# Bringing a recurrent state back to token layout: DVE 32x32 squares and a trip through DRAM in place of PE transposes

## The chip, the core and the metric

The kernel runs on one core of a Trainium2 chip. The metric is the device time of one launch in microseconds (us), of which the profiler gives a span (first to last instruction) and, for each engine, what it did when. The engines are named as in the profile: PE (TensorE, matrix multiply), PEld (its weight loads, which run beside the multiplies), DVE (VectorE), ACT (ScalarE), POOL (GpSimd) and SP (SyncE, which here only issues DMAs). Each engine works through its own list of instructions in order and waits on semaphores for the others.

## The reference

Four graph layers are applied to 32 graphs of 512 nodes with 128 features, all float32, over one adjacency matrix `adj` of 512x512. Each is `x = x + layer(relu(layernorm(x)))`. Layer 0 is a graph convolution, layer 1 a gated recurrent network of five steps, layers 2 and 3 are attention layers. The change touches layer 1 alone:

```python
def step(h, _):
    m_in = jnp.einsum('nm,bmd->bnd', in_matrix, h)      # both matrices are adj here
    m_out = jnp.einsum('nm,bmd->bnd', out_matrix, h)
    av = jnp.concatenate([m_in, m_out], axis=-1)
    u3 = h @ u3_w.T + u3_b
    z = jax.nn.sigmoid(av @ w3_w.T + w3_b + u3)
    r = jax.nn.sigmoid(av @ w4_w.T + w4_b + u3)
    hv = jnp.tanh(av @ w5_w.T + w5_b + (r * h @ u5_w.T + u5_b))
    h = (1.0 - z) * h + z * hv
    return (h, None)
h, _ = jax.lax.scan(step, input, None, length=5)
...
h = jnp.maximum(_layernorm(x, axis=-1), 0.0)
x = x + _L1_gnn_ref(h, adj, adj, ...)
```

The state `h` of a graph is 512 nodes by 128 features. The product with `adj` sums over nodes, the gates sum over features.

## The kernel before

**Layouts.** TensorE sums over partitions, so the state is kept twice: in token layout `h` (partition = node within a block of 128, then 4 blocks, then 128 features; C = 4 blocks) for the product with `adj`, and in feature layout `hT` (partition = feature, then 512 nodes) for the gates. The recurrence itself is computed in feature layout; `hT` has to be brought back to token layout once per step, for the next step's product, and after the last step for the sum `x += h - 1` (the 1 is taken off here because the elu of the next layer is added further on without its -1).

**A step of the recurrence** is four functions. `ggnn_prod` (L227) multiplies `h` as the stationary operand by `adjT` in four accumulating matmuls of 512 columns (L189) and copies the sum to `m` on ACT (L231). `ggnn_reset` (L234) runs two matmuls for the reset gate (L237, L238), tanh on ACT (L240) and one DVE operation giving `rh` (L242). `ggnn_update` (L245) adds to the same PSUM bank for the update gate (L247), tanh on ACT (L249), runs two matmuls for the candidate (L251, L252; the second needs `rh`), tanh on ACT (L254), then three DVE operations (L255, L256, L258), of which the last writes the new `hT`. `ggnn_back` (L261) brings it back to tokens: four TensorE transposes of 128x128 into the PSUM bank `back` (L264, recorded at the helper's line L184), and either an ACT copy to a new `h` (L267) or, after the last step, a DVE operation that adds it to `x` (L272).

**Order.** The order is written out at the end of the function (L344 to L364). Time is divided into slots `t`. Each slot holds one step of one graph (its product), the gates of the graph whose product was in the slot before, and the return to tokens of the graph whose product was two slots before; four graphs (LANES) are in flight, and a graph's next product comes four slots after the last one. Beside that each slot has pieces of the other layers (the list `side`): per graph the graph convolution (`gcn_in`, `gcn_prod`, `gcn_out`), the entry to the recurrence (`ggnn_in`, `ggnn_turn`), and for each of the two attention layers `gat_in`, `gat_heads`, `gat_edges`, `gat_out`. Five slots make a period, after which one more graph is through. Only in the first and last dozen slots are some of them empty. The framework in which it is written builds each engine's list from this and may move instructions against each other by its own planning; buffers rotate in pools: seven for `h`, eight for `hT`, two for a work tile where nothing is said, two PSUM banks called `side`, one tile of two banks called `wide`.

**What else is used below.** `ggnn_in` (L215) writes the first `h` with four ACT operations (L179). `ggnn_turn` (L220) transposes it to `hT` on TensorE (L184, `side<-ident,h`). `gat_heads` transposes its input (L184, `side<-ident,y`), copies it on DVE (L293, `gT`), and multiplies it (L296, `wide`). The output of a graph leaves by one DMA on SP's queue (L340).

Of the kernel before, what the change touches and what calls it, by code (L numbers as in the profile page):

```python
# [8 lines left out]
F32 = mybir.dt.float32  # L9
BF16 = mybir.dt.bfloat16  # L10
AF = mybir.ActivationFunctionType
ALU = mybir.AluOpType

P = 128
EPS = 1e-5
STEPS = 5
SLOPE = 0.2
LANES = 4


@with_exitstack
def gnn_stack(ctx: ExitStack, tc: tile.TileContext, a: dict, out: bass.AP):
    nc = tc.nc
    x, adj = a["x"], a["adj"]
    B, N, D = x.shape
    C = N // P
# [7 lines left out]
    def bank(name, bufs=1):  # L34
        return psum.tile([P, C, P], F32, name=name, bufs=bufs)

    def side_bank():
        return bank("side", 2)
# [4 lines left out]
    def flat(t):  # L43
        return t.rearrange("p c k -> p (c k)")
# [32 lines left out]
    xs = []  # L77
# [12 lines left out]
    for m in range(C):  # L90
        p = side_bank()
# [20 lines left out]
    for m in range(C):  # L112
        nc.vector.scalar_tensor_tensor(anT[:, m, :], anT[:, m, :], dinv[:, m:m + 1], flat(drow),
                                       op0=ALU.mult, op1=ALU.mult)
# [31 lines left out]
    for l in (2, 3):  # L146
# [5 lines left out]
        p = side_bank()  # L152
# [4 lines left out]
    work = ctx.enter_context(tc.tile_pool(name="work", bufs=2))  # L157
# [15 lines left out]
    def norm_relu(b, y):  # L173

        mv, rstd = norm_stats(b)
        off = stat.tile([P, C], F32, name="off")
        nc.vector.scalar_tensor_tensor(off, mv[:, :, 0], -1.0, rstd, op0=ALU.mult, op1=ALU.mult)
        for c in range(C):
            nc.scalar.activation(y[:, c, :], xs[b][:, c, :], AF.Relu, bias=off[:, c:c + 1],  # L179
                                 scale=rstd[:, c:c + 1])  # L180

    def to_features(p, y):
        for c in range(C):
            nc.tensor.transpose(p[:, c, :], y[:, c, :], ident)  # L184

    def product(p, h, mT):

        for c in range(C):
            nc.tensor.matmul(flat(p), h[:, c, :], mT[:, c, :], start=(c == 0), stop=(c == C - 1))  # L189

    kept = {}


# [19 lines left out]


    def ggnn_in(b):  # L215
        h = work.tile([P, C, D], F32, name="h", bufs=LANES + 3)
        norm_relu(b, h)
        kept["h", b] = h

    def ggnn_turn(b):  # L220
        p = side_bank()
        to_features(p, kept["h", b])
        hT = work.tile([P, N], F32, name="hT", bufs=2 * LANES)
        nc.scalar.copy(hT, flat(p))
# [20 lines left out]
    def ggnn_update(b, s):  # L245
# [10 lines left out]
        nc.vector.scalar_tensor_tensor(hv, z, 1.0, hv, op0=ALU.add, op1=ALU.mult)  # L256
        new = work.tile([P, N], F32, name="hT", bufs=2 * LANES)
        nc.vector.scalar_tensor_tensor(new, hv, 0.5, hT, op0=ALU.mult, op1=ALU.add)  # L258
        kept["hT", b] = new

    def ggnn_back(b, s):  # L261
        hT = kept["hT", b]
        p = bank("back")
        to_features(p, hT.rearrange("p (c k) -> p c k", c=C))  # L264
        if s < STEPS - 1:
            h = work.tile([P, C, D], F32, name="h", bufs=LANES + 3)
            nc.scalar.copy(flat(h), flat(p))  # L267
            kept["h", b] = h
        else:
            del kept["hT", b]  # L270

            nc.vector.scalar_tensor_tensor(flat(xs[b]), flat(xs[b]), -1.0, flat(p), op0=ALU.add, op1=ALU.add)  # L272

# [67 lines left out]

    span = LANES * (STEPS - 1)  # L344
    side = [(-8, gcn_in), (-7, gcn_prod), (-6, gcn_out), (-5, ggnn_in), (-4, ggnn_turn)]
    for i, l in enumerate((2, 3)):
        for k, f in enumerate((gat_in, gat_heads, gat_edges, gat_out)):
            side.append((span + 3 + 4 * i + k, lambda b, f=f, l=l: f(b, l)))

    def turn(t):  # L350
        s = -t % STEPS
        b, rest = divmod(t - LANES * s, STEPS)
        return (b, s) if rest == 0 and 0 <= b < B else None
# [3 lines left out]
    for t in range(first, last + 1):  # L357
        for lag, f in ((1, ggnn_reset), (0, ggnn_prod), (2, ggnn_back), (1, ggnn_update)):
            if (i := turn(t - lag)) is not None:
                f(*i)  # L360
        for k, f in side:
            b, rest = divmod(t - k, STEPS)
            if rest == 0 and 0 <= b < B:
                f(b)  # L364
# [30 lines left out]
```

The softmax here doesn't subtract the row's maximum and nothing guards it: scores larger than these inputs give would overflow.

## Time and profile before

| | |
|---|---|
| runs | 1884.26 us median of 3 (1883.15 to 1886.05) |
| profiled execution | 1884.31 us, span 1882.5 us |
| PE busy | 1832.7 us, 97% of the span |
| PEld busy | 1052.9 us, 56% |
| DVE busy | 1039.3 us, 55% |
| ACT busy | 723.8 us, 38% |
| POOL busy | 184.7 us, 10% |
| DMA, all queues | 19.88 MB, mean 11 GB/s |
| granted TensorE clock | 0.992 |

Busy times are of the whole span, with overlaps of one engine's instructions counted once. A float32 matmul appears as two records, a transpose as one. The recorded duration of a matmul runs past the start of the next, since they are pipelined: the time that one takes of the engine is the distance from its start to that of the next. After a vertical bar the tables of groups give busy time and mean duration, and after a second bar the engine's idle time just ahead of the group with what ended it.

### The profile page before, as it was taken

Reading aid. Unit: us, or ns where it says so; the run is one execution under the profiler, and the core shown is the slowest. Engines: PE = TensorE matmul, PEld = TensorE weight load, DVE = VectorE, ACT = ScalarE, POOL = GpSimd, SP = SyncE. Lnnn points to the kernel's source line nnn. Section 1 sums busy time; section 2 is a strip of 40 time slices with the busy share of each in tenths; the row PEclk is TensorE's granted clock in tenths of the full one; section 3 lists DMA queues with packets and bytes.
Section 4 is the critical chain, followed back from the end, with each engine's and each line's share of the span. In section 5 each row is a group of like instructions: output and inputs, shape, how many; then the busy total and the mean of one; then the engine's idle time right before and its main releaser. Section 6 shows DMA issues by size and latency. Waiting matters only on the chain.

```text
span 1882.5 us, 19768 instructions
## 1 busy us (share of the span) xinstructions
PE 1832.7 (97%) x7264; PEld 1052.9 (56%) x7264; DVE 1039.3 (55%) x2814; ACT 723.8 (38%) x1453; POOL 184.7 (10%) x168
## 2 busy tenths in 40 slices
PE   4999999999999999999999999999999999999995
PEld 2444556555556555556555556555555555555664
DVE  3334565555565555555565556565556565555665
ACT  2444443443343444343444344344344344333321
POOL 1101010110010111011111011111011011000000
PEclk9999999999999999999999999999999999999997
DMA  8000000000000000000000000000000000000000
GB/s 218 1 1 1 0 6 7 6 1 6 6 6 7 6 1 6 6 6 7 6 1 6 6 6 6 6 1 6 7 6 7 6 1 6 6 6 6 6 12 12
DMA packets 37056, 19.88 MB, mean 11 GB/s; under 512 B 2528, under 2 KB 36448, under 8 KB 36960
## 3 DMA queue, kind: packets, MB, share of 16 engines
q1 hardware_dynamic: 34368, 17.83, 3.3%
q8 instruction: 57, 0.93, 0.2%
q10 hardware_dynamic: 2592, 0.79, 0.2%
q14 instruction: 39, 0.32, 0.1%
HBM read 10.23 MB, written 8.39 MB: 10 GB/s over the span
## 4 chain that ended last, share of the span: by engine, by line
PE 96%; DVE 2%; DMA 1%; ACT 1%; issue 0%; POOL 0%; SPq 0%; ACTq 0%; DVEq 0%; POOLq 0%
PE prod L189 29%; PE wide L323 12%; PE gate L247 7%; PE cand L252 7%; PE gate L237 7%; PE cand L251 7%; PE gate L238 7%; PE side L189 6%; PE back L184 4%; PE wide L296 3%; PE side L184 2%; PE side L211 2%; PE side L311 1%; DMA x<-in_x_dram 1%; DMA u<-in_L_gnn_u_w_dram 0%
## 5 line engine op out<-in xcount | busy, mean ns | idle before, releaser
L189 PE MATMUL prod<-adjT,h 128*128 128x512 f32 x1280 | 583.2, 594 | 0.0
L189 PEld LDWEIGHTS prod<-adjT,h 128*128 128x128 f32 x1280 | 240.4, 191 | 285.7 <-issue 285.6
L255 DVE TENSOR_TENSOR hv<-hv,hT 128x512 f32<-128x512 f32 x160 | 111.0, 694 | 481.8 <-ACT hv L254 481.8
L170 POOL TENSOR_TENSOR rstd<-ve,mhalf 128x4 f32<-128x4 f32 x128 | 129.4, 1011 | 1557.4 <-DVE off L282 973.0
L323 PEld LDWEIGHTS wide<-h_gat,e 128*128 128x128 f32 x2048 | 238.3, 193 | 20.5 <-issue 11.6
L323 PE MATMUL wide<-h_gat,e 128*128 128x129 f32 x2048 | 241.8, 276 | 3.5 <-DVE o L338 1.5
L231 ACT COPY m<-prod 128x512 f32<-128x512 f32 x160 | 93.1, 582 | 328.6 <-PE prod L189 328.6
L240 ACT ACTIVATE r<-gate,gate_bw 128x512 f32<-128x512 f32 x160 | 109.9, 687 | 277.4 <-PE gate L238 273.6
L314 DVE SCALAR_TENSOR_TENSOR e<-side,h_gat,maskT 128x512 f32<-128x512 f32 x256 | 183.6, 741 | 4.2 <-PE side L311 4.0
L242 DVE SCALAR_TENSOR_TENSOR rh<-r,hT 128x512 f32<-128x512 f32 x160 | 109.4, 684 | 106.2 <-ACT r L240 106.0
L237 PE MATMUL gate<-m,w4T 128*128 128x512 f32 x320 | 164.2, 595 | 2.0 <-ACT m L231 1.5
L247 PE MATMUL gate<-m,w3T 128*128 128x512 f32 x320 | 164.3, 595 | 0.2 <-ACT r L240 0.2
L252 PE MATMUL cand<-rh,u5T 128*128 128x512 f32 x320 | 163.5, 592 | 0.3 <-DVE rh L242 0.3
L238 PE MATMUL gate<-hT,u3T 128*128 128x512 f32 x320 | 163.4, 592 | 0.0
L251 PE MATMUL cand<-m,w5T 128*128 128x512 f32 x320 | 163.4, 592 | 0.0
L254 ACT ACTIVATE hv<-cand,gate_bw 128x512 f32<-128x512 f32 x160 | 109.1, 682 | 97.2 <-PE cand L252 96.8
L258 DVE SCALAR_TENSOR_TENSOR hT<-hv,hT 128x512 f32<-128x512 f32 x160 | 134.7, 842 | 2.6 <-DVE arg L298 0.2
L184 PEld LDWEIGHTS back<-ident,hT 128*128 128x128 f32 x640 | 79.8, 141 | 84.8 <-issue 81.9
L285 ACT ACTIVATE y<-x,off 128x128 f32<-128x128 f32 x256 | 87.7, 393 | 92.7 <-DVE off L282 92.7
L249 ACT ACTIVATE z<-gate,gate_bw 128x512 f32<-128x512 f32 x160 | 109.5, 684 | 27.9 <-PE gate L247 27.9
L164 DVE BATCH_NORM_STATS2 st<-x 128x6 f32<-128x128 f32 x512 | 119.0, 280 | 1.2
L189 PE MATMUL side<-anT,y 128*128 128x512 f32 x256 | 117.4, 601 | 1.9 <-ACT y L179 1.9
(93 smaller groups left out, 1625.8 us busy)
## 6 DMA issues: line engine op xcount, KB each, us to landing
x<-in_x_dram SPq DMA_DIRECT2D x32, 256.0 KB, 5.4
out_dram<-o SPq DMA_DIRECT2D x32, 256.0 KB, 2.2
adj_sb<-in_adj_dram SPq DMA_DIRECT2D x4, 256.0 KB, 5.3
w<-in_L_gnn_w_w_dram ACTq DMA_DIRECT2D x3, 128.0 KB, 5.6
u<-in_L_gnn_u_w_dram ACTq DMA_DIRECT2D x2, 64.0 KB, 4.5
w<-in_L_gnn_W_dram ACTq DMA_DIRECT2D x1, 64.0 KB, 3.0
b<-in_L_gnn_b_dram ACTq DMA_DIRECT2D x1, 64.0 KB, 5.4
w_aug<-in_L_gnn_W_dram ACTq DMA_DIRECT2D x1, 64.0 KB, 3.7
```

The lines of the kernel that those rows point to most:

```text
L164: nc.vector.bn_stats(st[:, c, :], xs[b][:, c, :])
L170: nc.gpsimd.tensor_tensor(rstd, ve, mhalf, ALU.pow)
L184: nc.tensor.transpose(p[:, c, :], y[:, c, :], ident)
L189: nc.tensor.matmul(flat(p), h[:, c, :], mT[:, c, :], start=(c == 0), stop=(c == C - 1))
L237: nc.tensor.matmul(flat(p), wT["w4"], m, start=True, stop=False)
L238: nc.tensor.matmul(flat(p), wT["u3"], hT, start=False, stop=True)
L247: nc.tensor.matmul(flat(p), wT["w3"], m, start=False, stop=True, skip_group_check=True)
L251: nc.tensor.matmul(flat(q), wT["w5"], m, start=True, stop=False)
L252: nc.tensor.matmul(flat(q), wT["u5"], rh, start=False, stop=True)
L258: nc.vector.scalar_tensor_tensor(new, hv, 0.5, hT, op0=ALU.mult, op1=ALU.add)
L314: nc.vector.scalar_tensor_tensor(e[:, j, :], flat(row), h[:, j, D + 1:D + 2], maskT[l][:, j, :], op0=ALU.max, op1=ALU.mult)
L323: nc.tensor.matmul(p[:, c, :D + 1], e[:, j, c * P:(c + 1) * P], h[:, j, :D + 1], start=(j == 0), stop=(j == C - 1))
```

## The change

The return to token layout leaves TensorE. DVE transposes `hT` in squares of 32x32 within each group of 32 partitions, which puts each feature group's squares into `sq`; four DMAs, one for each group of 32 partitions, write `sq` to a scratch tensor in DRAM in which the four feature groups of a token stand side by side; a fifth DMA reads that as the new `h`. All five are on SP's queue, and the fifth waits for the four. The tile `h` now has the features outside and the four blocks inside, so that a block's features are 16 bytes apart for all who write or read it: the ACT operations of `ggnn_in`, the stationary operand of the product and of `ggnn_turn`, and the sum at the end. That sum now reads `h` from SBUF and no longer a PSUM bank.

```diff
+W = 32
+Q = P // W
...
+    dram = ctx.enter_context(tc.tile_pool(name="dram", bufs=1, space=bass.MemoryType.DRAM))
+
+    def to_tokens(h, hT):
+        sq = work.tile([P, Q, W, C], F32, name="sq")
+        nc.vector.transpose(sq.rearrange("p q j c -> p q c j"), hT.rearrange("p (c q i) -> p q c i", c=C, q=Q))
+        d = dram.tile([Q, W, Q, W * C], F32, name="squares", bufs=4)
+        for a in range(Q):
+            nc.sync.dma_start(d[:, :, a, :].rearrange("q i k -> i q k"),
+                              sq[a * W:(a + 1) * W].rearrange("i q j c -> i q (j c)"))
+        nc.sync.dma_start(h.rearrange("p j c -> p (j c)"), d.rearrange("q i a k -> (q i) (a k)"))
...
     def ggnn_in(b):
-        h = work.tile([P, C, D], F32, name="h", bufs=LANES + 3)
+        h = work.tile([P, D, C], F32, name="h", bufs=LANES + 3).rearrange("p d c -> p c d")
         norm_relu(b, h)
...
     def ggnn_back(b, s):
         hT = kept["hT", b]
-        p = bank("back")
-        to_features(p, hT.rearrange("p (c k) -> p c k", c=C))
+        h = work.tile([P, D, C], F32, name="h", bufs=LANES + 3)
+        to_tokens(h, hT)
+        h = h.rearrange("p d c -> p c d")
         if s < STEPS - 1:
-            h = work.tile([P, C, D], F32, name="h", bufs=LANES + 3)
-            nc.scalar.copy(flat(h), flat(p))
             kept["h", b] = h
         else:
             del kept["hT", b]
-            nc.vector.scalar_tensor_tensor(flat(xs[b]), flat(xs[b]), -1.0, flat(p), op0=ALU.add, op1=ALU.add)
+            nc.vector.scalar_tensor_tensor(xs[b], xs[b], -1.0, h, op0=ALU.add, op1=ALU.add)
```

In the changed file the lines lie 14 or 15 lower: the square is L199, the writes L202, the read L204, the last sum L286.

## The prediction

> **What bounds the kernel now.** First the page's busy shares and its chain of work that ended last:
>
> ```profile
> PE 1832.7 (97%) x7264; PEld 1052.9 (56%) x7264; DVE 1039.3 (55%) x2814; ACT 723.8 (38%) x1453; POOL 184.7 (10%) x168
> ...
> PE 96%; DVE 2%; DMA 1%; ACT 1%; issue 0%; POOL 0%; SPq 0%; ACTq 0%; DVEq 0%; POOLq 0%
> ```
>
> PE is the bound, and a busy PE can still hide gaps, so I read one period (five slots) in the timeline of PE. It starts at 1000.13 and the next at 1056.40: 56.27 us without a gap, five times with the work that the change removes:
>
> ```profile
> 1001.85 3.60 PE L189 MATMUL prod<-adjT,h 128*128 128x512 f32 x8
> 1005.28 0.60 PE L184 MATMUL back<-ident,hT 128*128 128x128 f32 x4
> 1005.72 1.02 PE L247 MATMUL gate<-m,w3T 128*128 128x512 f32 x2
> ...
> 1032.02 1.06 PE L296 MATMUL wide<-w_aug,gT 128*128 128x131 f32 x8
> ...
> 1039.36 1.02 PE L252 MATMUL cand<-rh,u5T 128*128 128x512 f32 x2
> ```
>
> A group of four transposes holds PE from 1005.28 to 1005.72, 0.44 us. A time taken off PE is therefore a gain as long as DVE still delivers `gT` before 1032.02, `rh` before 1039.36, and so on. DVE's timeline of the same period:
>
> ```profile
> 1005.92 0.69 DVE L272 SCALAR_TENSOR_TENSOR x<-x,back 128x512 f32<-128x512 f32 x1 [0.63 <-PE back L184]
> ...
> 1009.40 0.69 DVE L255 TENSOR_TENSOR hv<-hv,hT 128x512 f32<-128x512 f32 x1 [1.33 <-ACT hv L254]
> ...
> 1014.43 0.69 DVE L242 SCALAR_TENSOR_TENSOR rh<-r,hT 128x512 f32<-128x512 f32 x1 [2.88 <-ACT r L240]
> ...
> 1030.92 0.69 DVE L293 COPY gT<-side 128x512 f32<-128x512 f32 x1 [0.99 <-PE side L184]
> ...
> 1037.72 0.67 DVE L242 SCALAR_TENSOR_TENSOR rh<-r,hT 128x512 f32<-128x512 f32 x1
> ```
>
> `gT` is done at 1031.61, 0.41 us ahead of its matmul; the last `rh` at 1038.39, 0.97 ahead. Between 1030.92 and 1037.72 DVE has no idle time: this stretch, not its 55%, decides. For the DMAs, two rows of issues:
>
> ```profile
> out_dram<-o SPq DMA_DIRECT2D x32, 256.0 KB, 2.2
> adj_sb<-in_adj_dram SPq DMA_DIRECT2D x4, 256.0 KB, 5.3
> ```
>
> The first is a store on an idle queue, the second a load like the new one (128 rows of 2 KB) with three others in flight; its fastest took 2.9 us.
>
> **What the skill says.** *VectorE: DVE Perf Modes*, "The three transpose paths": DVE transposes squares of 32x32 only, 311 ns for 128x128 bf16. *SBUF — State Buffer*, "Specifications (TRN2)": cache lines of 16 bytes need two hits for full bandwidth; the new `sq` and `h` are walked at a step of 16 bytes, one hit each. No row of before walks a large tile so. *TensorE: Matmul & The Clock Gate*, "What happens when you issue a matmul": weight loads are pulled ahead of running matmuls, at columns/1.2 ns, 107 ns for 128; the trace's transposes stand 0.44/4 = 0.109 us apart, which agrees. Its Part 1 says that PE's clock halves after some 3.4 us of idling: after a wait of 4.1 us at 41.02 the stretch from 40 to 60 us has a mean clock of 0.84, against 1.00 before it.
>
> **The change part by part.** All against the profiled execution, 1884.3 us (span 1882.5 and 1.8 around it), which is the median of the runs to 0.05 us.
>
> *Removed from PE.* 160 groups; 2 lie where the head waits and 6 in the tail after 1775 us (counted below), so 152 x 0.438 = **-66.6 us**. Also 128 ACT copies (L267, 592 ns, 75.7 us): nothing by themselves, ACT is idle 62% of the time. The bank `back` is of no use to others.
>
> *The square on DVE, 160.* For contiguous data 311 ns + 384 further elements: L338 (344 ns for 128 elements, PSUM input) and L133 (291 ns) against 691 ns for 512 put one element near 1.0 ns, so about 0.69 us, the price of any 128x512 operation here. At half rate on the 16-byte write side, 0.16 fixed + 512 x 2.08 ns = 1.22 us. Both ends stay; I take 1.22, from the page's remark. In a dense stretch neighbours lasting 0.69 start 0.60 apart, so a square adds 0.60 to 1.13. By the built order one square falls between DVE's `hv` at 1020.82 and `gT` at 1030.92, where DVE's own work ends at 1029.92: +1.13 gives 1031.05. PE asks for `gT` 0.44 earlier than before, 1030.48. DVE is 0.57 late, 0.41 is to spare, and the weight load after `gT` needs some 0.2: PE waits 0.36 per period. About 30 periods: **+11 us** (0 at 0.69). The next square stands behind the last `rh`, and that keeps 0.3 of its 0.97. The three others fall into idle time of 0.7 to 2.9 us.
>
> *The trip.* SP issues in 0.372 us each (the store's issue): the fourth write starts 1.12 after the square, lands at most 2.2 later; the read takes 2.9; hand-overs 0.1: 6.3 us, from 5 (smaller writes land sooner) to 9 (the load's 5.3). For steps one to four the product comes some 20 us after the square in the built order, so it is hidden with 13 to spare; SP is otherwise idle, and one trip in five has a store of an output between its writes (1.3 us). After the last step DVE itself waits: square 999.6 to 1000.8, data at 1007.1, where the sum (L286) before began at 1005.92. Queued behind it: layer norm statistics, `hv`, and `rh` at 1014.43. The 1.33 and 2.88 us of idle time ahead of these take it up; from the start of L286 to that `rh` DVE has 6.7 us of work (L286 at half rate 1.22, statistics 1.6, three operations 2.1, a square 1.13, `rh` 0.69) and PE wants it near 1018.0 (1019.04 before, two groups of transposes earlier now, less the weight load), so L286 may start at 1011.3 and the trip last 10.5 us. Cost 0.
>
> *Strided `h`.* Each of a slot's 8 weight loads for the product has a matmul record of 0.43 us (3.43/8) over it; at half rate, 0.21 us, it stays hidden. `ggnn_turn`'s four transposes are only as long as their loads: +0.11 each, 3 exposed, 30 graphs: **+10 us** (0 at full rate). ACT's four writes of 494 ns grow by 0.13 at most, in the place of the copies removed.
>
> *The head.* In the first slots there is little to hide a trip behind. The first new `hT` was done at 62.78 and its product began at 64.17. Now 62.8 + 1.2 + 6.3 = 70.3, and by the built list an `anT` matmul stands ahead of the product and waits for DVE's statistics until about 71: 7 us late, of which 1.3 is filled with a turn and that matmul, and PE's clock costs some 2 after the gap: 8. The product at 82.49 waits likewise: its read stands on SP's queue behind two writes of the next square (about 93.5), so it lands near 97, while PE has work until 92.3: 5 with the clock's 1.5, less the idle 1.1 that this stretch had. With two returns saved **+13 us** (8 to 20).
>
> *The tail.* After 1775 us the slots are half empty, and three places wait for a return; I followed the built lists of PE and DVE through them with the durations above. DVE is in order: L286 waits for its trip, and `hv`, the next square, and `gT` for the attention layer stand behind it. The product of the 31st graph's last step and the attention work around it, done 30.1 us after the 30th's last candidate matmul, come to 34.2 (+4.1); the 32nd graph's last product +2.8; the last sum (back at 1835.82, L272 at 1836.85) comes 8 us later, but DVE's work for the other graph runs first and the matmuls after it move by 2.5. With 0.6 for the clock **+10 us** (6 to 18; each us more of trip costs 1 to 3 here and 2 in the head).
>
> Sum: -66.6 + 11 + 10 + 13 + 10 = -22.6; **1861.7 us**, 1.2% faster.
>
> **The rivals.**
> *A, no price for the step of 16 bytes:* squares 0.69, loads hidden: -66.6 + 12 + 8.6 = -46, **1838 us**. For it: the page gives no size of the penalty. Against: the remark itself.
> *B, dear weight loads, slower:* the step makes a load of `h` four times as long. In 30 periods the turns lose 90 x (L - 0.109) us, and the products 1200 x (L - 0.43) beyond 0.43. With the rest as forecast the gain of 22.6 (and the 10 that the turns have in it) is gone at L = 0.43 us: 90 x 0.32 = 29 and a little. At 0.45 it is 1861.7 - 10 + 31 + 24, **1906 us**. For it: nothing in this trace loads weights at a step. Against: PEld is 56% busy and idle for 285.7 us ahead of the product's 1280 loads, 0.22 each.
> *C, the trip stops DVE:* beyond 10.5 us each further us costs 32; at 11.2 the gain is gone, at 12 **1910 us**. Against: the store lands in 2.2 us, the queues are empty.
> *D, squares slower than half rate:* 1.9 us would give 0.7 more per period, and **1883 us**.
> That PE keeps its work cannot be: the built list has no such transposes.
>
> **How the numbers follow.** Forecast 0.52, A 0.24, B 0.08, C 0.06, D 0.05 and a head and tail at their upper ends together with the forecast's costs 0.05 (1876). Forecast and A are faster; C and most of B slower; D near the border. By the 0.2% (3.8 us) that a measurement of this kernel can tell: faster 0.77, same 0.05, slower 0.18. The forecast's own range is 1846 to 1877; with A below and D above, 1834 to 1888.
>
> **What would show it.** Right: a PE period near 54.4 us (56.27 - 2.19 + 0.36) with no `back`; squares near 1.2 us; issue of the first write to landing of the read near 6; L286 waiting about 1 us on a DMA; PE waits on a DMA of `h` only before 100 and after 1775 us; waits of `wide` (L310) on `gT`. Wrong: transposes of `ggnn_turn` or the products standing further apart (B); `hv` or `rh` late after L286 (C); long squares (D). The forecast is most easily spoiled by the size of the 16-byte penalty, which nothing here measures.

## The result and the profile after

The changed kernel takes 1885.36 us (median of 4 runs, 1883.74 to 1886.61) against 1884.17 for the kernel before: a ratio of 1.0005, with a 95% interval of 0.9987 to 1.0022. The forecast of 1861.7 us did not come. TensorE did lose its 160 groups of transposes, and the span is still 1882.0 us instead of 1882.5.

First the page of the changed kernel: the busy times, the chain, the row of the square with its mean duration after the comma, and the DMA issues with the time to landing in the last column.

```profile
PE 1786.1 (95%) x6624; PEld 1147.9 (61%) x6624; DVE 1194.8 (63%) x2974; ACT 663.4 (35%) x1325; POOL 172.5 (9%) x168
...
PE 68%; DVE 19%; issue 5%; POOL 3%; ACT 3%; DMA 1%; SPq 0%; DVEq 0%; ACTq 0%; POOLq 0%
...
L199 DVE STREAM_TRANSPOSE sq<-hT 128x512 f32<-128x512 f32 x160 | 175.9, 1100 | 1.3
...
squares<-sq SPq DMA_DIRECT2D x640, 64.0 KB, 1.8
h<-squares SPq DMA_DIRECT2D x160, 256.0 KB, 2.6
```

PE's share of the chain fell from 96% to 68%, and DVE's rose from 2% to 19%: the end is now set in part by work that PE waits for. One period of PE's timeline, to be read against the one shown of the kernel before:

```profile
1001.16 3.60 PE L191 MATMUL prod<-adjT,h 128*128 128x512 f32 x8
1004.59 1.02 PE L262 MATMUL gate<-m,w3T 128*128 128x512 f32 x2
...
1022.23 1.06 PE L310 MATMUL wide<-w_aug,gT 128*128 128x131 f32 x8
1023.12 2.85 PE L191 MATMUL prod<-adjT,h 128*128 128x512 f32 x6
1025.81 1.02 PE L262 MATMUL gate<-m,w3T 128*128 128x512 f32 x2
...
1036.17 1.02 PE L266 MATMUL cand<-m,w5T 128*128 128x512 f32 x2
1038.26 1.12 PE L267 MATMUL cand<-rh,u5T 128*128 128x512 f32 x2 [1.08 <-DVE rh L257]
```

No transposes stand after the product any more. The period lasts 55.56 us (the mean over a hundred products in the middle), 0.71 less than the 56.27 of before, where five groups of 0.438 should have given 2.19. Two losses are in these rows. The six records of the product after `wide` take 2.69 us (1023.12 to 1025.81) where they took 2.58 in the kernel before (1024.69 to 1027.27, two rows further down). And `cand<-rh` could have started at 1036.17 + 0.86 = 1037.03 and starts at 1038.26, 1.23 late (the row says 1.08, since the recorded end of a matmul runs past the next start); a weight load exposed behind this wait adds 0.11. Together that is 1.45, and 1.48 with 0.03 for the turn: what the period lacks. The two rows of the kernel before:

```profile
1024.69 2.74 PE L189 MATMUL prod<-adjT,h 128*128 128x512 f32 x6
1027.27 0.60 PE L184 MATMUL back<-ident,hT 128*128 128x128 f32 x4
```

In all, PE of the changed kernel waits for `rh` 27 times, about once a period; the columns are total, count and longest:

```profile
PE cand L267 <- DVE rh L257: 27.3, 27, 1.1
...
PE prod L191 <- DMA h<-squares: 4.3, 1, 4.3
```

Over the whole run, from the starts of the 160 products compared with before: the fourth product is 15.6 us late (what comes up to it is the head), the 157th is 13.9 early (so the middle gained 29.5 of the 67 that 153 groups are), and the end is 0.5 early (so the tail lost 13.4).

Why `rh` is late shows when the engines are read together, here the changed kernel from the candidate matmul two slots before it:

```profile
1027.53 1.02 PE L267 MATMUL cand<-rh,u5T 128*128 128x512 f32 x2
1028.39 0.60 PE L186 MATMUL side<-ident,y 128*128 128x128 f32 x4
...
1029.10 0.16 DVE L179 SCALAR_TENSOR_TENSOR off<-mv,rstd 128x4 f32<-128x4 f32 x1 [1.12 <-POOL rstd L172]
...
1029.29 1.26 ACT L181 ACTIVATE y<-x,off,rstd 128x128 f32<-128x128 f32 x3 [1.73 <-DVE off L179]
...
1030.46 0.67 ACT L269 ACTIVATE hv<-cand,gate_bw 128x512 f32<-128x512 f32 x1
...
1031.16 0.69 DVE L270 TENSOR_TENSOR hv<-hv,hT 128x512 f32<-128x512 f32 x1 [1.30 <-ACT hv L269]
...
1037.53 0.68 DVE L257 SCALAR_TENSOR_TENSOR rh<-r,hT 128x512 f32<-128x512 f32 x1
```

ACT could have begun `hv` when its matmul was done at 1028.39. But three of the four relus of the graph convolution's `y` stand ahead of it in ACT's list, and they wait for `off`, the end of a layer norm on DVE and POOL, which DVE begins at 1029.10 and ends at 1029.26. So ACT idles 1.73 us and `hv` begins at 1030.46; DVE, in order too, then works without idle time from its own `hv` to `rh`. In the kernel before these relus stood behind `hv`:

```profile
1029.39 1.26 ACT L179 ACTIVATE h<-x,off,rstd 128x128 f32<-128x128 f32 x3
1030.55 0.68 ACT L254 ACTIVATE hv<-cand,gate_bw 128x512 f32<-128x512 f32 x1
1031.12 1.65 ACT L179 ACTIVATE y<-x,off,rstd 128x128 f32<-128x128 f32 x4
```

There `hv` began 0.27 after its matmul was done (at 1030.28), and now 2.07 after. No line of the diff touches `hv` or `y`: the framework planned ACT's list anew around the changed work. The kernel before had nothing of this kind to gain: from 200 to 1700 us its PE is busy for 1500.0 us.

### The profile page after: what moved, and what is told of

The parts are those of the page before. It is cut to its first block, busy times and chain, and to the rows that moved or that the text cites. A ratio compares the mean times of both kernels' runs of the same rounds, so it can differ in the third digit from the quotient of the medians.

```text
span 1882.0 us, 19825 instructions
## 1 busy us (share of the span) xinstructions
PE 1786.1 (95%) x6624; PEld 1147.9 (61%) x6624; DVE 1194.8 (63%) x2974; ACT 663.4 (35%) x1325; POOL 172.5 (9%) x168
## 3 DMA queue, kind: packets, MB, share of 16 engines
q1 hardware_dynamic: 149568, 101.77, 20.4%
## 4 chain that ended last, share of the span: by engine, by line
PE 68%; DVE 19%; issue 5%; POOL 3%; ACT 3%; DMA 1%; SPq 0%; DVEq 0%; ACTq 0%; POOLq 0%
PE prod L191 20%; PE wide L337 12%; PE cand L267 6%; PE side L191 6%; PE gate L262 5%; PE gate L253 5%; PE cand L266 5%; PE gate L252 5%; DVE hT L273 3%; POOL rstd L172 3%; DVE e L328 3%; DVE hv L271 2%; DVE h_gat L318 2%; PE side L186 2%; DVE st L166 1%
## 5 line engine op out<-in xcount | busy, mean ns | idle before, releaser
L191 PEld LDWEIGHTS prod<-adjT,h 128*128 128x128 f32 x1280 | 392.4, 309 | 172.2 <-issue 40.8
L267 PE MATMUL cand<-rh,u5T 128*128 128x512 f32 x320 | 166.5, 602 | 27.3 <-DVE rh L257 27.3
L199 DVE STREAM_TRANSPOSE sq<-hT 128x512 f32<-128x512 f32 x160 | 175.9, 1100 | 1.3
L267 PEld LDWEIGHTS cand<-rh,u5T 128*128 128x128 f32 x320 | 58.2, 189 | 112.9 <-issue 59.7
L166 DVE BATCH_NORM_STATS2 st<-x 128x6 f32<-128x128 f32 x512 | 122.8, 280 | 1.3
```

Of the source, the lines that this page charges most:

```text
L166: nc.vector.bn_stats(st[:, c, :], xs[b][:, c, :])
L199: nc.vector.transpose(sq.rearrange("p q j c -> p q c j"), hT.rearrange("p (c q i) -> p q c i", c=C, q=Q))
L267: nc.tensor.matmul(flat(q), wT["u5"], rh, start=False, stop=True)
```

## The experiments

The theory is that this order on ACT loses the middle's gain, and that head and tail are trips that nothing hides. The first rival is the square: it makes DVE's dense stretch too long, whatever ACT does.

**1. `hv` first.** The relus of the graph convolution's `y` are queued behind the `hv` of the third step before, and no row of any other engine's list moves. Its line numbers are one or two higher.

```diff
-    def norm_relu(b, y):
+    def norm_relu(b, y, behind=None):
...
-        for c in range(C):
...
+        with tc.issue_after(behind) if behind is not None else ExitStack():
+            for c in range(C):
...
     def gcn_in(b):
...
-        norm_relu(b, y)
+        norm_relu(b, y, hvs[-3] if len(hvs) > 4 else None)
...
-        nc.scalar.activation(hv, flat(q), AF.Tanh, bias=gate_b["w5"])
+        hvs.append(nc.scalar.activation(hv, flat(q), AF.Tanh, bias=gate_b["w5"]).ins)
```

> Only ACT's order changes: the four relus of the graph convolution's y are queued behind the tanh hv of the third step before, as they stood in the kernel before; the lists of PE, DVE, SP and POOL stay as in the changed kernel. Theory (the loss of the middle is hv standing on ACT behind relus that wait for DVE's off): hv comes about 1.9 us sooner, PE's waits for rh at L267 of the changed kernel (27.3 us in 27 places) fall below 5 us, the period goes from 55.56 to about 54.4 us, and the time to 1885.4 - 29 x 1.19 (1.08 of waiting and 0.11 of a weight load after it) = 1851 us (1845 to 1858). Rival (the square makes DVE's dense stretch too long, whatever ACT does): PE still waits over 20 us for rh, and the time stays within 1880 to 1886 us.

Measured: 1849.81 us (1849.71 to 1852.14), 0.9826 of the kernel before (0.9810 to 0.9843). The same place in its timeline:

```profile
1007.55 1.02 PE L269 MATMUL cand<-rh,u5T 128*128 128x512 f32 x2
1008.61 0.69 ACT L271 ACTIVATE hv<-cand,gate_bw 128x512 f32<-128x512 f32 x1 [1.03 <-PE cand L269]
...
1010.75 1.23 ACT L182 ACTIVATE y<-x,off,rstd 128x128 f32<-128x128 f32 x3
...
1015.02 0.69 DVE L259 SCALAR_TENSOR_TENSOR rh<-r,hT 128x512 f32<-128x512 f32 x1
1017.04 1.02 PE L269 MATMUL cand<-rh,u5T 128*128 128x512 f32 x2
```

`hv` begins 0.20 us after its matmul (done at 1008.41), `rh` is done at 1015.71, and PE takes it at 1017.04, 1.33 later, as soon as it is free. All waits for `rh` together are 0.3 us, and the period is 54.22. The theory's number came (1851), the rival's did not. The recorded waits of 27.3 us, with 0.15 each for the recorded end and 0.11 each for the weight load, are 34.3 us; the two spans differ by 34.1 (1882.0 and 1847.9), the two medians by 35.6.

**2. The length of the square.** What the 16-byte step costs is taken away: `sq` is written contiguously, so the tokens of `h` are in the wrong places. Once with ACT's order as in the changed kernel, once with `hv` first.

```diff
-        nc.vector.transpose(sq.rearrange("p q j c -> p q c j"), hT.rearrange("p (c q i) -> p q c i", c=C, q=Q))
+        nc.vector.transpose(sq.rearrange("p q j c -> p (q j c)"), hT)
```

> The square writes sq contiguously and not at a step of 16 bytes (so h is no longer in token order, that is left out); no list of any engine changes. Both expect the square to last 0.7 instead of 1.10 us. Theory (hv late through ACT's order): off, then y, then hv come 0.4 us sooner, no more, so the waits for rh fall by 0.4 each, and the time by 29 x 0.4 = 12 and some 1 in the head: 1872 us (1868 to 1876). Rival (the half-rate square is itself the loss of the middle): the wait for rh goes as a whole, 1850 us.

> Both edits at once: contiguous square (h not in token order) and y behind hv on ACT. Theory: with hv in time, the square's 0.4 us lie in slack, so this is at most 3 us (head and tail) below the kernel with y behind hv alone: 1849 us if that one is at 1851. Rival (the square's length is the loss): this and the contiguous square alone are equal, within 4 us.

Measured: 1872.66 us (1872.28 to 1873.14) with the old order and 1847.87 (1847.25 to 1848.48) with `hv` first. In the first, square and waits for `rh` are:

```profile
L199 DVE STREAM_TRANSPOSE sq<-hT 128x512 f32<-128x512 f32 x160 | 111.7, 698 | 1.3
```

```profile
PE cand L267 <- DVE rh L257: 17.7, 25, 0.7
```

With a square of 0.70 instead of 1.10, `off`, and with it the relus and `hv`, come earlier, and each wait is shorter by nearly that: the longest goes from 1.1 to 0.7, the period from 55.56 to 55.20. With `hv` first the same 0.40 brings 1.9 us in all, and the period is 54.22 as without it. So the square's length counts only through the order on ACT.

**3. No square at all.** The writes take `hT` itself, so `h` is again not in token order; trip and strided `h` stay.

```diff
-        sq = work.tile([P, Q, W, C], F32, name="sq")
-        nc.vector.transpose(sq.rearrange("p q j c -> p q c j"), hT.rearrange("p (c q i) -> p q c i", c=C, q=Q))
...
-                              sq[a * W:(a + 1) * W].rearrange("i q j c -> i q (j c)"))
+                              hT[a * W:(a + 1) * W].rearrange("i (q k) -> i q k", q=Q))
```

> The changed kernel without the square: the four writes read hT itself (h is then not in token order, that is left out); trip and strided h stay. Nothing is queued by hand, and in the list that the framework then plans for ACT, hv stands ahead of y as in the kernel before. Theory (square and ACT's order together are the middle's loss; the trip and the strided h cost nothing there): no waits for rh, the time of the kernel with contiguous square and hv first, 1847.9 us, less 0 to 4 for trips that start 0.7 us sooner in head and tail: 1846 us (1842 to 1850). Rival (the wait for rh comes with the DMAs or the strided reading of h, which stay): over 15 us of waits for rh, 1865 us or more.

Measured: 1885.71 us (1883.74 to 1886.79, 14 runs), 1.0013 of the kernel before (1.0004 to 1.0021): 40 us above the theory's number, with 15.5 us of waits for `rh` in 25 places, as the rival had said. Its timeline:

```profile
1028.52 1.02 PE L265 MATMUL cand<-rh,u5T 128*128 128x512 f32 x2
...
1029.18 0.16 DVE L179 SCALAR_TENSOR_TENSOR off<-mv,rstd 128x4 f32<-128x4 f32 x1 [1.12 <-POOL rstd L172]
...
1029.38 0.49 ACT L181 ACTIVATE y<-x,off,rstd 128x128 f32<-128x128 f32 x1 [1.80 <-DVE off L179]
...
1029.78 0.67 ACT L262 ACTIVATE z<-gate,gate_bw 128x512 f32<-128x512 f32 x1
...
1030.50 0.30 PEld L250 LDWEIGHTS gate<-m,w4T 128*128 128x128 f32 x2 [0.33 <-ACT z L262]
...
1031.52 0.66 ACT L267 ACTIVATE hv<-cand,gate_bw 128x512 f32<-128x512 f32 x1
```

The expectation had misread the planned list: three relus of `y` do stand behind `hv`, but the first stands ahead of `z`, waits 1.80 us for `off`, and pushes `z`, three relus of `h` and `hv` behind it: `hv` begins 2.14 us after its matmul (done at 1029.38). PE pays twice: of the 1.24 us by which this period (55.47) exceeds 54.22, 0.89 is the wait for `rh` with its weight load, and the rest is the next reset gate's first matmul (L250), which waits for the late `z`. Since the planner moved rows on DVE and PE as well, this kernel alone does not decide between that relu and the rival's DMAs. So only the relus of `y` were moved in it:

> The kernel without a square (h not in token order, that is left out), with the four relus of y queued behind hv. In its predecessor one relu of y stood ahead of z and waited 1.80 us for off; that is the only thing moved: 42 rows of ACT's list, none of another engine. Theory (a relu waiting for off ahead of z and hv is enough to lose the gain, square or not): the waits for rh (15.5 us in 25 places) go, the period falls by 1.25 to about 54.2 us, and the time to 1885.7 - 29 x 1.25 = 1849 us (1845 to 1853). Rival (without the square it is the DMAs or the strided h that make rh late): over 10 us of these waits stay, 1870 us or more.

Measured: 1850.12 us (1849.73 to 1851.75), 0.9828 (0.9812 to 0.9845), no wait for `rh`, `hv` begins 0.24 after its matmul, period 54.22. The DMAs and the strided `h` stayed, so they are not the cause of these waits. A single relu that waits for `off` ahead of `z` and `hv` is enough to lose the gain, even where DVE is busy for 1056.2 us and not 1194.8; and with `hv` first the square, 1.1 us in each slot, costs nothing that shows in the period.

**4. The ends.** In the three kernels of this part `y` stays behind `hv`, and some returns go by PE transposes again, the rest by square and trip (a turn is the slot in which a return's product stood):

```diff
     def ggnn_back(b, s):
         hT = kept["hT", b]
+        if not 4 < STEPS * b + LANES * s < STEPS * B + 1:
+            p = bank("back")
+            to_features(p, hT.rearrange("p (c k) -> p c k", c=C))
+            if s < STEPS - 1:
+                h = work.tile([P, D, C], F32, name="h", bufs=LANES + 3).rearrange("p d c -> p c d")
+                nc.scalar.copy(h, p)
+                kept["h", b] = h
+                return
+            del kept["hT", b]
+            nc.vector.scalar_tensor_tensor(flat(xs[b]), flat(xs[b]), -1.0, flat(p), op0=ALU.add, op1=ALU.add)
+            return
```

The condition shown is the last kernel's. First a wide choice:

> y behind hv as in the first, and the returns of the first 7 turns (up to turn 12) and of the last 20 (from turn 145 on) go back to PE transposes with an ACT copy or a sum from PSUM; the 133 between keep squares and trip. Theory (the head's +15.6 and the tail's +13.4 us are trips that nothing hides): both come back, less 27 groups of 0.438 us on PE of which some 8 lie in idle time: 1851 - 29 + 8 = 1830 us (1824 to 1838), no PE wait of over 2 us on a DMA of h or on gT, y in head and tail. Rival (much of the ends' loss is the stalled clock or strided operands): at most half comes back, 1843 us or more.

Measured: 1834.9 us (1830.96 to 1837.94), in the theory's range. The starts of the products showed that few of the 27 returns had been in anybody's way, hence two narrower choices:

> y behind hv on ACT, and only the returns of turns 0 and 4 (the first graph's first two steps) go by PE transposes; 158 squares stay. Theory (the head's loss is two products that wait for these two trips): the fourth product starts within 1 us of the kernel before and not 14.7 us later, the time is 1849.8 - 14 = 1836 us (1832 to 1840). Rival (the wait passes on to the trips of turns 5 and 8): the fifth or sixth product is still 6 us or more late, 1842 us or more.

> The same, and the last six returns (turns 161 to 171) by PE transposes as well; 152 squares stay. Theory (of the tail's 14 us, from the 157th product to the end, nearly all hangs on these six trips): 1836 - 14 + 2 for the transposes on PE = 1824 us (1820 to 1830). Rival (the returns just before, turns 154 to 159, then stop DVE or PE in the tail): a third or more of the 14 us stays, 1829 us or more, as with the 27 returns on PE (1834.9), and PE shows waits of over 2 us after the start of the 157th product.

Measured: 1837.94 us (1837.20 to 1838.94) with the two of the head, where the fourth product now starts 0.6 us later than before and not 14.7; and 1825.76 (1824.42 to 1827.26) with the six of the tail as well, 0.9695 of the kernel before (0.9680 to 0.9709). So two returns by square and trip cost the head 12 us net, and six cost the tail 12. What happened in the head is seen in the changed kernel:

```profile
90.06 4.96 SPq L202 DMA_DIRECT2D squares<-sq  x6
...
95.18 0.34 SPq L204 DMA_DIRECT2D h<-squares  x1
...
98.06 5.27 PE L191 MATMUL prod<-adjT,h 128*128 128x512 f32 x8 [4.32 <-DMA h<-squares]
```

SP issues six writes before the read: four of its square, and two of the next one, which is done only at 94.22 (its row on DVE begins at 93.13 and lasts 1.09). So the read goes out 5.1 us after the first write, where the trip before it, with four writes ahead, took 3.2 (64.23 to 67.39), and the product waits 4.32 us; its row of eight then lasts 5.27 instead of 3.60, in a stretch (98 to 104 us) whose granted clock is 0.73, against 1.00 from 80 to 98.

The last kernel of the three is 57 us below the kernel before, with 152 of 160 returns off PE.

## Why the prediction was wrong, point by point

- **What bounds the kernel: right.** PE was the bound, and each group taken off it is worth 0.438 us once nothing else is late: with `hv` first the period is 54.22, which is 56.27 - 2.19 + 0.14.
- **"The next square stands behind the last `rh`, and that keeps 0.3 of its 0.97": this step failed.** That `rh` came 1.2 us too late for PE. The sentence took ACT's list to be the old one: the working follows the planned lists of PE and DVE and the queue of SP, and the three relus moved ahead of `hv` stand in ACT's, which it doesn't follow. It is not a size but a missing term of the sum, put at nothing and worth some 34 us. The middle was forecast at -66.6 + 11 + 10 = -45.6 and came to -29.5: the two costs put down there, 21 us together, came to 4, and the missing term is the rest. Putting those two 17 us too high nearly halved the miss, and that was luck. Rival D had 1883 us from squares of 1.9 us; they lasted 1.10, and the second experiment excludes that cause.
- **The square, +11: too much.** It lasts 1.10 us (ends 0.69 and 1.22), and in the middle PE waits for `gT` only once, for 0.25 us at 202 us. This step of the forecast added 1.13 to a stretch of DVE and left out that it begins with an `hv` that PE releases; that `hv` now comes at 19.80 us of the period and not at 20.69, two groups of transposes earlier.
- **The trip, 0 in the middle: right.** The square is done at 1000.07 and L286 begins at 1005.89: 5.8 us, forecast 6.3. L286 waits 1.0 us, as forecast, and the idle time behind it took that up:

```profile
998.97 1.10 DVE L199 STREAM_TRANSPOSE sq<-hT 128x512 f32<-128x512 f32 x1
...
1005.89 1.10 DVE L286 SCALAR_TENSOR_TENSOR x<-x,h 128x512 f32<-128x512 f32 x1 [1.03 <-DMA h<-squares]
```

That a trip of up to 10.5 us would still cost nothing wasn't tried.

- **Strided weight loads, +10 at the turn: wrong place.** They take 309 ns on average (191 before) for the product and are hidden there; the turn's four transposes take 0.47 us instead of 0.44, under 1 us in all. What they probably do cost was not foreseen: the 0.11 per period after `wide`, about the size by which a load grew; no run took the step away there, so this is inferred.
- **Head +13 and tail +10: low in size, at 15.6 and 13.4; the mechanism right in the head, in the tail in part.** The queue of SP in the head did what was written, and the read of the fourth product landed in time for 98.06 where the working had about 97. In the tail `gT` does stand behind the last sum and a square on DVE, and PE waits for it:

```profile
1806.48 2.11 PE L310 MATMUL wide<-w_aug,gT 128*128 128x131 f32 x8 [4.16 <-DVE gT L307]
```

But L286 does not wait for its trip there, as the working had it: its rows at 1802.87 and 1835.08 begin without idle time. The kernel without squares and with `hv` first loses 15.3 us in the same stretch, so the squares' time alone is not it. That six returns by PE bring 12 us back is measured; whether the trips themselves or the order planned around them cost it stays open.

- **The rivals.** A's 1838 and B's 1906 did not come; A's loads were hidden as it said. The case that came, no change, was held to be a 1 in 20 chance, since the unread list was in none of the cases. The chances are also not added up rightly: by the cases named, faster comes to 0.81 and slower to 0.14 at most, where 0.77 and 0.18 are written.

The sum as measured, from the product starts: -67.0 for 153 groups in the middle, +37.5 lost there again, +15.6, +13.4: -0.5 us, the difference of the spans. The order of ACT is shown to be the cause by runs. Why the planner set the relus there is not settled.

## What to carry to other kernels

Where a framework plans the lists, an edit can move instructions that it does not touch: compare the lists of all engines before and after, and look above all for an operation that waits for something new ahead of one that the bound engine needs. A small operation that is only early, not urgent, can be queued behind the urgent one by hand; here that brought some 34 us. A long trip in place of a short operation cost nothing in the full middle here and 12 us at each end, so try the short way for the first and last few turns.

## What the hardware showed that was not expected

- **At a step of 16 bytes DVE took about 60% longer, not 100%.** A square of 512 float32 per partition took 1.10 us written at that step and 0.70 written contiguously (where `hT` was also read straight through); the last sum took 1.108 us reading `h` at that step from SBUF, against 0.687 with its operand contiguous in PSUM. The Trainium skill (*SBUF — State Buffer*, "Specifications (TRN2)") speaks of two hits of a 16-byte line for full bandwidth; half rate was the guess drawn from that, and the measurement decides.
- **Other engines at that step.** An ACT relu of 128 columns writing `h` took 598 ns (494 before); a weight load of 128x128 for the product 309 ns (191 before).
- **The trip is short.** A write of 64 KB landed 1.8 us after its issue and the read of 256 KB in 2.6, though 84 MB more went through the DMA engines than before (103.8 against 19.9); SP's queue took 20.4% of the 16 engines' time.
